# Attention phase: how fill products are paced, how much is kept for the next unit, and how VectorE's side list is ordered

## The chip, the cores and the metric

The kernel runs on one core of one Trainium2 chip. A core has TensorE (PE, matrix products; its weight loads are PEld), VectorE (DVE), ScalarE (ACT), GpSimd (POOL), SyncE (SP, which here issues DMAs), and DMA engines. The metric is device time in microseconds, the median of several runs. One further execution was profiled, and every duration below is from that one.

## The reference

Four sequences of 1024 tokens, 512 features, float32. Cut to what matters:

```python
x = x + xattn(layernorm(x), ctx, ctx)
x = x + ffn(layernorm(x))

# xattn: 16 heads of 32
q, k, v = heads(x @ Wq.T), heads(ctx @ Wk.T), heads(ctx @ Wv.T + bv)
scores = q @ k.T / sqrt(32)
mask = triu(ones, k=0); mask[0, 0] = False      # key s may be seen by queries t > s
probs = softmax(where(mask, -inf, scores))
out = (probs @ v) @ Wo.T + bo

# ffn: 128 experts each choose one token of every group of 32
logits = x @ controller + tie
perm = logits == max(logits over the 32 tokens)
out = combine(relu(dispatch(x, perm) @ f1 + bias) @ f2, perm)
```

The change lies in the first line, the attention. The expert part is left as it is.

## The kernel before

**Units.** `attention_phase` works in 16 units; a unit is one batch b and one group hc of four heads (u = 4 b + hc). The main loop (L581) runs u from -1 to 15. A round works on two units at once: it computes the scores of unit u+1, to find each query's maximum, and the softmax and output of unit u. A round has twelve steps k:

- `score_piece(u+1, k)` (L312; PE L325, masks L331): the scores of 128 queries against up to 512 keys, queries on the partitions, into two score buffers (tile sc); VectorE takes the negative maxima out of them (L337, tile nm). The pieces have 128, 256, 384, 512, 512, 128, 512, 256, 512, 384, 512, 512 columns.
- `key_block(u, k)` (L366; PE L381, L387): the same scores again, with keys on the partitions, into two score buffers (tile st), the maxima being subtracted by a product with a row of ones (L387, which reads mxT); ScalarE takes the exponential (L395, tile pr), GpSimd zeroes what is masked on the diagonal (L398). The blocks have 512, 384, 256, 128, then 512 four times, then 512, 384, 256, 128 queries. Here the first four belong to the first half of the queries, the other eight to the second.
- `weigh_values` (L422; PE L431, tile av), two steps behind: the probabilities times v.
- `add_sums` (L404): adds the probabilities up for the softmax's denominator, one half on GpSimd, the other on VectorE (L415, L418).
- At the end of a half of the queries `normalize` (L444): the denominator (pd, L449), its reciprocal on VectorE (L456), its spreading (pb, L460), and the multiplication into atT (L464).

There are three score buffers, so a score piece and a key block always wait for each other's readers. All other products share one PSUM buffer, ps_m.

**The maxima.** `split_maxima` (L341) writes the maxima as a sum of three bf16 numbers (five small VectorE operations, L348 to L353, and L345 first for the second half); PE then turns them (pmx, L358) and VectorE copies them to mxT (L361), which `key_block` reads. It is begun after piece 4 for the first half and after piece 11 for the second: VectorE's five operations are placed at once, and PE's turn becomes due 3.0 us later by the kernel's own reckoning.

**The fill.** Between score pieces and key blocks stand products for other units, each a generator that yields after every product of 0.86 us: q and k of unit u+2 (L207, L195), v of unit u+1 (L226), the rows of the output product of the batch before (L266, called o; VectorE adds the residual, L272), and in two of four rounds the turning of the next batch's normalized rows (L171, called x). They stand in one list, `fill`. `ensure` (L533) forces the list on until a named step is done, for example the q and k that the next piece reads. The planner keeps estimated clocks (`now`, `dve`, `act`, and `bank`, the time at which ps_m is free again). `slot` (L502) is called twice per step:

```python
owed[0] += credit                    # total of the round's fill / 24
while owed[0] > 0 or now[0] < until:
    if open_step[0] is None:
        if now[0] < bank[0]:
            return
        open_step[0] = choose(False)
```

So each round's fill is spread over its 24 slots, and nothing is meant to remain. The order that comes out is kept: the phase runs under a manual schedule for PE, VectorE, ScalarE and GpSimd. SP is not among them.

**The side list.** `aside` (L114) holds work for VectorE that is not urgent: the layer norm of the next batch (`measure`, L139 and L140, four times, an empty entry, then `center`, L150) and the moments of finished rows (`measure_row`, L254). Each step of a round takes one entry, whatever its length.

Of the kernel before, what the change touches and what calls it, by code (L numbers as in the profile page):

```python
# [14 lines left out]
ALU = mybir.AluOpType  # L15
# [22 lines left out]
def attention_phase(  # L38
# [74 lines left out]

    aside = deque()  # L114

    x_t = x.rearrange("b (h t p) d -> b h p t d", p=P, t=4)

    def ln_steps(b):
# [12 lines left out]
        def measure(half, i):  # L131
            if i == 0:
                stats[half] = (
                    spool.tile([P, 6], F32, tag="ln_stats", name=f"ln_stats_{b}_{half}"),
                    spool.tile([P, 4, 2], F32, tag="ln_mv", name=f"ln_mv_{b}_{half}"),
                    spool.tile([P, 4], F32, tag="ln_rstd", name=f"ln_rstd_{b}_{half}"),
                )
            st, mv, rstd = stats[half]
            nc.vector.bn_stats(st, held[half][:, i, :])  # L139
            nc.vector.bn_aggr(mv[:, i, :], st)  # L140
            given(dve, 1.0)
            if i == 3:
                nc.vector.tensor_scalar_add(rstd, mv[:, :, 1], EPS)
                nc.gpsimd.tensor_tensor(rstd, rstd, mhalf, ALU.pow)

        def center(t):
            half, i = divmod(t, 4)
            st, mv, rstd = stats[half]
            xn = qpool.tile([P, D], F32, tag="xn", name=f"xn_{b}_{t}")
            nc.vector.tensor_scalar(  # L150
                xn, held[half][:, i, :], mv[:, i, 0:1], rstd[:, i : i + 1],
                ALU.subtract, ALU.mult,
            )
            given(dve, 0.6)
            ready[t] = xn

        def prepare(half):
            for i in range(4):
                aside.append(lambda i=i: measure(half, i))
            aside.append(lambda: None)  # L160
            aside.append(lambda: center(4 * half))

        def step(t):
            while t not in ready:
                aside.popleft()()
            if t % 4 < 3:
                center(t + 1)
            xn = ready.pop(t)
            px = single([P, NC, P], f"px_{b}_{t}")
            for c in range(NC):  # L170
                nc.tensor.transpose(px[:, c, :], xn[:, ts(c, P)], ident)  # L171
            yield 4 * SMALL, act, 0.6
            nc.scalar.copy(xnTs[b][:, :, ts(t, P)], px)  # L173
# [68 lines left out]

    def load_residual(b, t):
        xt = opool.tile([P, D], F32, tag="xr", name=f"xr_{b}_{t}", bufs=3)
        nc.sync.dma_start(xt, x[b, ts(t, P), :])
# [6 lines left out]
    def measure_row(b, t, x2):  # L252
        st = opool.tile([P, 6], F32, tag="row_stats", name=f"row_stats_{b}_{t}", bufs=2)
        nc.vector.bn_stats(st, x2)  # L254
        nc.vector.bn_aggr(moments[:, b * NT + t, :], st)
        given(dve, 1.0)

    def o_step(b, t, ahead=None):
# [14 lines left out]
        nc.sync.dma_start(x2_dram[ds(b * S + t * P, P), :], xt)  # L273
        aside.append(lambda: measure_row(b, t, xt))

# [65 lines left out]
    def split_maxima(u, half):  # L341

        nm = nms.pop((u, half))
        if half == 1:
            nc.vector.tensor_tensor(nm[:, 0], nm[:, 0], nm[:, 1], ALU.min)  # L345
        mxs = mxs_tiles[half]
        n = nm[:, 0]
        nc.vector.tensor_copy(mxs[:, :, :, 0], n)  # L348
        rest = spool.tile([P, 4, R], F32, tag="rest", name=f"rest_{u}_{half}")
        nc.vector.tensor_tensor(rest, n, mxs[:, :, :, 0], ALU.subtract)  # L350
        nc.vector.tensor_copy(mxs[:, :, :, 1], rest)
        nc.vector.tensor_tensor(rest, rest, mxs[:, :, :, 1], ALU.subtract)
        nc.vector.tensor_copy(mxs[:, :, :, 2], rest)  # L353
        given(dve, 1.0)
        yield None
        pt = ps_m.tile([P, 4, P], BF16, tag="pm", name=f"pmx_{u}_{half}")
        for i in range(4):
            nc.tensor.transpose(pt[:, i, :], mxs[:, i].rearrange("p r m -> p (r m)"), ident16)  # L358
        yield 0.3, dve, 0.4
        mxT = spool.tile([P, HS], BF16, tag=f"mxT{half}", name=f"mxT_{u}_{half}", bufs=1 + half)  # L360
        nc.vector.tensor_copy(mxT, pt.rearrange("p i q -> p (i q)"))  # L361
        mxTs[u, half] = mxT

# [105 lines left out]


    fill, soon, done = deque(), deque(), set()
    open_step, owed = [None], [0.0]

# [5 lines left out]
    def advance(step):  # L479
# [4 lines left out]
        now[0] += part[0]  # L484
        owed[0] -= part[0]
        if len(part) == 1:
# [7 lines left out]
    def choose(force):  # L494
        for i in range(len(soon)):
            if soon[i][0] <= now[0] or (force and not fill):
                step = soon[i][1]
                del soon[i]
                return step
        return fill.popleft()[1] if fill else None  # L500

    def slot(credit, until=0.0):  # L502

        owed[0] += credit
        if owed[0] > 0 or now[0] < until:
            now[0] += TURN
        while owed[0] > 0 or now[0] < until:
            if open_step[0] is None:
# [13 lines left out]

    def named(steps, costs, *names):


        def noted(step, name):
            yield from step
            done.add(name)

        for step, cost, name in zip(steps, costs, names):  # L530
            fill.append((cost, noted(step, name)))

    def ensure(*names):  # L533
        while not done.issuperset(names):
            one_part()

    def begin(step, wait):

        next(step)
        soon.append((now[0] + wait, step))  # L540

# [11 lines left out]
    for half in range(2):  # L553
        ln_prepare(half)
        while aside:
            aside.popleft()()
        run(k_first[half])
# [14 lines left out]
    def add(kind, u, steps, cost=4 * LARGE, first=0):  # L572
        named(steps, [cost] * len(steps), *((kind, u, first + n) for n in range(len(steps))))

# [6 lines left out]
    for u in range(-1, NU):  # L581
# [6 lines left out]
        if b > 0:  # L588
            if hc == 0:
                load_residual(b - 1, 0)  # L590
            ends = (3, 6, 8, 8) if more else (2, 4, 8, 8)
            r0 = ends[hc - 1] if hc else 0
            rows = o_todo(b - 1, r0, ends[hc])
        if more and hc == 1:
            next_ln = ln_steps(b + 1)
            next_ln[0](0)
            aside.append(lambda: None)
            next_ln[1](0)
# [6 lines left out]
        elif more and hc == 2:  # L605
            ensure(("x", b + 1, 3))
            next_ln[0](1)
            aside.append(lambda: None)
            next_ln[1](1)
# [8 lines left out]
        else:  # L618
# [3 lines left out]
            add("o", b - 1, rows, first=r0)  # L622
        total = sum(cost for cost, _ in fill) + 4.0
        owed[0] = 0.0
        for k in range(STEPS):
            if u + 1 < NU:
# [3 lines left out]
                if k == 4:  # L630
                    begin(split_maxima(u + 1, 0), 3.0)
                if k == STEPS - 1:
                    begin(split_maxima(u + 1, 1), 3.0)
            weighed = False
            slot(total / (2 * STEPS), scores_free() if u >= 0 else 0.0)
            if u >= 0 and len(pending) == LAG and now[0] < scores_free():
                pending.popleft()()
                weighed = True
            if u >= 0:
                h, j = blocks[k]  # L640
                while (u, h) not in mxTs:
                    one_part()
                key_block(u, k)
            if sums:
                sums.popleft()()
            if aside:
                aside.popleft()()
            if len(pending) == LAG and not weighed:
                pending.popleft()()
            if u >= 0:  # L650
# [15 lines left out]
                pending.append(weigh)  # L666
            slot(total / (2 * STEPS), scores_free() if u + 1 < NU else 0.0)
    while sums:
# [3 lines left out]
    while soon or fill or open_step[0]:  # L672
        one_part()
    while aside:
        aside.popleft()()
    units.close()
# [387 lines left out]
```

## Time and profile before

| | us |
|---|---|
| three runs, median (lowest to highest) | 1543.44 (1539.7 to 1546.15) |
| the profiled execution, whole | 1544.16 |
| its span, first to last instruction | 1542.5 |
| mean granted TensorE clock | 0.961 |
| first score piece of the phase (L325) | 41.1 |
| last spreading of a denominator (L460) | 1204.1 |

From about 1206 us on the routing and the experts follow. Busy time by stage, from the windows view:

| stretch, us | PE busy | VectorE | ScalarE | GpSimd | PE clock |
|---|---|---|---|---|---|
| 200 to 400 | 190.11 | 117.65 | 63.29 | 69.36 | 0.97 |
| 400 to 600 | 195.56 | 119.13 | 60.36 | 75.79 | 0.97 |
| 600 to 800 | 197.15 | 117.14 | 58.84 | 73.90 | 0.99 |
| 800 to 1000 | 193.58 | 117.03 | 62.95 | 68.76 | 0.97 |
| 1140 to 1220 | 69.45 | 45.44 | 29.28 | 54.40 | 0.89 |

How to read the profile: busy time is the time in which an engine executes; matmuls are pipelined, so a busy PE is not PE at its peak. A row of the groups has line, engine, operation, tiles, count, then busy time and mean duration, then the idle time before and what ended it. The letter in front of an arrow is what was waited for.

### The profile page before, as it was taken

How to read it: one execution, taken by the hardware profiler on the slowest of the kernel's cores; microseconds unless marked ns; L12 is line 12 of the kernel's file. 1: busy time of each engine (PE TensorE's matmuls, PEld its weight loads, DVE VectorE, ACT ScalarE, POOL GpSimd, SP SyncE). 2: the span in 40 equal slices, each digit the busy share in tenths (PEclk: the TensorE clock that was granted, in tenths of full speed). 3: DMA queues.
4: the chain of work that ended last, by engine and by line, in shares of the span. 5: the costliest groups of instructions: out<-in, count | busy, mean ns of one | idle time of the engine just before them, and what ended most of it. 6: DMA issues, size and time to landing. Idle time of an engine off the chain costs nothing.

```text
span 1542.5 us, 32131 instructions
## 1 busy us (share of the span) xinstructions
PE 1449.4 (94%) x14048; PEld 780.1 (51%) x14048; DVE 897.8 (58%) x1353; ACT 516.7 (33%) x809; POOL 479.1 (31%) x557
## 2 busy tenths in 40 slices
PE   6999989999999999999999999999998898987996
PEld 4343444444353444453535443535443456877886
DVE  3655656655565655646665655565576454575664
ACT  1033333332322233232323332322235123644663
POOL 1033333432424232424242433342447410000222
PEclk9999989999999899999998999999999797898998
DMA  8000001000000210001011000000011669653664
GB/s 290 17 1 1 1 28 55 29 1 1 21 21 22 75 56 28 1 1 35 8 42 56 28 1 1 2 28 1 28 35 49 208 244 319 181 159 123 187 210 141
DMA packets 77868, 105.64 MB, mean 68 GB/s; under 512 B 4128, under 2 KB 41504, under 8 KB 77600
## 3 DMA queue, kind: packets, MB, share of 16 engines
q1 hardware_dynamic: 75168, 95.20, 19.2%
q0 software_dynamic: 2560, 8.39, 1.7%
q8 instruction: 110, 1.80, 0.5%
q14 instruction: 30, 0.25, 0.0%
HBM read 74.22 MB, written 29.36 MB: 67 GB/s over the span
## 4 chain that ended last, share of the span: by engine, by line
PE 80%; DVE 7%; issue 6%; POOL 3%; DMA 2%; ACT 1%; POOLq 0%; SPq 0%; ACTq 0%; DVEq 0%
PE sc L325 11%; PE st L381 10%; PE av L431 8%; PE pq L207 8%; PE pv L226 8%; PE pk L195 7%; PE po L266 6%; PE pd L862 3%; DVE nm L337 3%; PE sc L331 3%; PE pi L881 2%; PE st L387 2%; PE po L713 2%; PE pl L750 2%; PE pd L449 2%
## 5 line engine op out<-in xcount | busy, mean ns | idle before, releaser
L337 DVE TENSOR_REDUCE nm<-sc 128x2 f32<-128x1024 f32 (+3 forms) x384 | 349.5, 952 | 296.8 <-PE sc L331 210.3
L395 ACT ACTIVATE pr<-st 128x1024 f32<-128x1024 f32 (+3 forms) x384 | 290.4, 808 | 587.4 <-PE st L387 577.0
L398 POOL TENSOR_SCALAR_AFFINE_SELECT pr<-pr 128x256 f32<-128x256 f32 x256 | 113.6, 452 | 469.3 <-ACT pr L395 467.7
L418 POOL TENSOR_TENSOR acc<-acc,pr 128x1024 f32<-128x1024 f32 (+3 forms) x128 | 209.2, 1634 | 115.0 <-ACT pr L395 106.9
L325 PE MATMUL sc<-kT,qT 32*128 32x512 f32 (+3 forms) x1536 | 202.0, 537 | 7.4 <-ACT pr L395 5.4
L381 PE MATMUL st<-qT,kT 32*128 32x512 f32 (+3 forms) x1536 | 196.8, 551 | 0.0
L431 PE MATMUL av<-pr,v 128*32 128x512 f32 (+3 forms) x1536 | 168.7, 508 | 6.4 <-POOL pr L398 6.0
L195 PE MATMUL pk<-ct,w_k 128*128 128x512 f32 x256 | 125.6, 620 | 9.2 <-DMA w_k<-in_wkT_dram 9.2
L226 PEld LDWEIGHTS pv<-w_v,ct 128*128 128x128 f32 x1024 | 118.7, 192 | 26.4 <-issue 13.3
L207 PE MATMUL pq<-xnT,w_q 128*128 128x512 f32 x256 | 128.3, 627 | 1.4 <-ACT xnT L173 1.4
L226 PE MATMUL pv<-w_v,ct 128*128 128x128 f32 x1024 | 128.3, 280 | 0.0
L381 PEld LDWEIGHTS st<-qT,kT 32*128 32x128 f32 x1536 | 67.5, 188 | 116.2 <-issue 89.5
L418 DVE TENSOR_TENSOR acc<-acc,pr 128x1024 f32<-128x1024 f32 (+3 forms) x128 | 119.6, 935 | 10.3 <-POOL pr L398 9.1
L325 PEld LDWEIGHTS sc<-kT,qT 32*128 32x128 f32 x1536 | 73.9, 186 | 101.0 <-issue 58.3
L415 POOL TENSOR_TENSOR acc<-pr,pr 128x768 f32<-128x768 f32 (+1 forms) x32 | 67.6, 2111 | 117.7 <-ACT pr L395 117.7
L979 POOL DMA_DIRECT2D out_dram<-xr x32 | 24.3, 758 | 253.4 <-DVE xr L978 253.1
L266 PE MATMUL po<-w_o,atT 128*128 128x512 f32 x192 | 94.9, 615 | 0.0
L195 PEld LDWEIGHTS pk<-ct,w_k 128*128 128x128 f32 x256 | 45.0, 192 | 71.1 <-issue 65.7
L431 PEld LDWEIGHTS av<-pr,v 128*32 128x32 f32 x1536 | 32.0, 109 | 88.7 <-issue 64.4
L207 PEld LDWEIGHTS pq<-xnT,w_q 128*128 128x128 f32 x256 | 45.5, 197 | 56.5 <-issue 51.8
L387 PE MATMUL st<-mxT,ones 32*128 32x512 bf16 (+3 forms) x768 | 72.9, 328 | 0.0
L456 DVE RECIPROCAL rd<-pd 128x128 f32<-128x128 f32 x32 | 30.5, 954 | 52.8 <-PE pd L449 52.8
(94 smaller groups left out, 1601.9 us busy)
## 6 DMA issues: line engine op xcount, KB each, us to landing
ct<-in_ctxT_dram SPq DMA_DIRECT2D x8, 1024.0 KB, 5.2
xt<-in_x_dram SPq DMA_DIRECT2D x8, 1024.0 KB, 5.3
xr<-in_x_dram SPq DMA_DIRECT2D x32, 256.0 KB, 2.6
xn_dram<-x SPq DMA_DIRECT2D x8, 1024.0 KB, 5.3
xn<-xn_dram SPq DMA_DIRECT2D x8, 1024.0 KB, 6.2
f<-in_f_dram SPq DMA_DIRECT2D x16, 512.0 KB, 4.3
xr<-x_dram SPq DMA_DIRECT2D x32, 256.0 KB, 4.4
f<-in_f_dram SPq DMA_DIRECT2D x32, 256.0 KB, 4.9
```

The source lines that it names most:

```text
L195: nc.tensor.matmul(pk, lhsT=weights["k"][:, c, ts(hc, P)], rhs=cts[b, half][:, c, :], start=(c == 0), stop=(c == NC - 1),)
L207: nc.tensor.matmul(pq, lhsT=weights["q"][:, c, ts(hc, P)], rhs=xnTs[b][:, c, ts(half, HS)], start=(c == 0), stop=(c == NC - 1),)
L226: nc.tensor.matmul(pv[:, t, :], lhsT=cts[b, half][:, c, ts(t, P)], rhs=weights["v"][:, c, ts(hc, P)], start=(c == 0), stop=(c == NC - 1),)
L266: nc.tensor.matmul(po, lhsT=atTs[b * NC + c][:, ts(t, P)], rhs=weights["o"][:, c, :], start=(c == 0), stop=(c == NC - 1),)
L325: nc.tensor.matmul(scs[r // 2][:, r % 2, :n], lhsT=qT[rr, ts(i, P)], rhs=kT[rr, ds(c0, n)], start=True, stop=not diag,)
L337: nc.vector.tensor_reduce(nm[:, c0 // HS, i % 4, ts(g, 2)], scs[g][:, :, :n], AX.X, ALU.max, negate=True)
L381: nc.tensor.matmul(scs[r // 2][:, r % 2, :n], lhsT=kT[rr, ts(j, P)], rhs=qT[rr, ds(h * HS + q0, n)], start=True, stop=False,)
L387: nc.tensor.matmul(scs[r // 2][:, r % 2, :n], lhsT=ones16[rr, :], rhs=mxT[rr, ds(q0, n)], start=False, stop=True,)
L395: nc.scalar.activation(pr[:, :, :n], scs[g][:, :, :n], AF.Exp)
L398: nc.gpsimd.affine_select(out=d, in_=d, compare_op=ALU.is_ge, fill=0.0, base=0 if j == 0 else -1, pattern=[[0, 2], [P + 1, P]], channel_mu ...
L418: engine.tensor_tensor(acc, acc, pr[:, :, :n], ALU.add)
L431: nc.tensor.matmul(avs[u, h][rr, q0:], lhsT=vs[u][:, j, rr], rhs=pr[r // 2][:, r % 2, : HS - q0], start=(j == 0), stop=(j == last),)
```

## The change

It touches the planner and the places in which VectorE's small work stands.

- `slot` gets the number of slots left in the round. It works on until the backlog of fill has shrunk by its share of what lies above a reserve of 5.0 us. The reserve stays in the list for the next round. The backlog is counted down product by product.
- Entries of the side list carry a name and a cost. `beside(0.9)` takes entries until their cost is 0.9 us or more, `finish` does named ones at once. The empty entries between the x load and its first measure are gone.
- The split of the maxima becomes two entries of the side list (0.9 and 0.7), put at its front. The second makes PE's turn due, 1.5 us later. Before a key block both are finished.
- A row's moments go to the front of the list; they are finished before the residual load that reuses their buffer.
- In the last batch's rounds the rows of the output product are spread as (2, 4, 7, 8) instead of (2, 4, 8, 8): one row moves to the last round.

```diff
-    aside = deque()
+    aside, pieces_left = deque(), {}
+
+    def later(name, cost, work, front=False):
+        pieces_left[name] = (cost, work)
+        if front:
+            aside.appendleft(name)
+        else:
+            aside.append(name)
+
+    def finish(*names):
+        for name in names:
+            if name in pieces_left:
+                cost, work = pieces_left.pop(name)
+                work()
+                given(dve, cost)
+
+    def beside(budget):
+        while aside and budget > 0:
+            name = aside.popleft()
+            if name in pieces_left:
+                budget -= pieces_left[name][0]
+                finish(name)
...
         def prepare(half):
             for i in range(4):
-                aside.append(lambda i=i: measure(half, i))
-            aside.append(lambda: None)
-            aside.append(lambda: center(4 * half))
+                later(("m", b, half, i), 1.0, lambda i=i: measure(half, i))
+            later(("pow", b, half), 1.0, lambda: None)
+            later(("c", b, half), 0.6, lambda: center(4 * half))
...
         def step(t):
-            while t not in ready:
-                aside.popleft()()
+            half = t // 4
+            finish(*(("m", b, half, i) for i in range(4)), ("c", b, half))
...
     def load_residual(b, t):
+        finish(("row", b, t - 3), ("row", b - 1, t + 5))
...
-        aside.append(lambda: measure_row(b, t, xt))
+        later(("row", b, t), 0.9, lambda: measure_row(b, t, xt), front=True)
...
     def split_maxima(u, half):
...
+        def first_two():
+            if half == 1:
+                nc.vector.tensor_tensor(n, n, nm[:, 1], ALU.min)
+            nc.vector.tensor_copy(mxs[:, :, :, 0], n)
+            nc.vector.tensor_tensor(rest, n, mxs[:, :, :, 0], ALU.subtract)
+            nc.vector.tensor_copy(mxs[:, :, :, 1], rest)
+
+        def third():
+            nc.vector.tensor_tensor(rest, rest, mxs[:, :, :, 1], ALU.subtract)
+            nc.vector.tensor_copy(mxs[:, :, :, 2], rest)
+            soon.append((now[0] + 1.5, turn()))
...
+        later(("split", u, half, 1), 0.7, third, front=True)
+        later(("split", u, half, 0), 0.9, first_two, front=True)
...
-    def slot(credit, until=0.0):
-
-        owed[0] += credit
-        if owed[0] > 0 or now[0] < until:
+    def slot(slots_left, until=0.0):
+
+        goal = backlog[0] - max(0.0, backlog[0] - RESERVE) / slots_left
+        if backlog[0] > goal or now[0] < until:
             now[0] += TURN
-        while owed[0] > 0 or now[0] < until:
+        while backlog[0] > goal or now[0] < until:
...
-            ends = (3, 6, 8, 8) if more else (2, 4, 8, 8)
+            ends = (3, 6, 8, 8) if more else (2, 4, 7, 8)
...
                 if k == 4:
-                    begin(split_maxima(u + 1, 0), 3.0)
+                    split_maxima(u + 1, 0)
                 if k == STEPS - 1:
-                    begin(split_maxima(u + 1, 1), 3.0)
+                    split_maxima(u + 1, 1)
...
-            slot(total / (2 * STEPS), scores_free() if u >= 0 else 0.0)
+            slot(2 * (STEPS - k), scores_free() if u >= 0 else 0.0)
...
                 h, j = blocks[k]
+                finish(("split", u, h, 0), ("split", u, h, 1))
                 while (u, h) not in mxTs:
                     one_part()
                 key_block(u, k)
             if sums:
                 sums.popleft()()
-            if aside:
-                aside.popleft()()
+            beside(0.9)
...
-            slot(total / (2 * STEPS), scores_free() if u + 1 < NU else 0.0)
+            slot(2 * (STEPS - k) - 1, scores_free() if u + 1 < NU else 0.0)
```

`turn`, not shown, is the former second half of `split_maxima`, unchanged: the four transposes and the copy to mxT.

## The prediction

> **What bounds the kernel now.** I read the page first. Its first section has TensorE (PE) busy for 94% of the span; the chain of waits gives PE 80%. PE is the bound of the attention phase (0 to about 1206 us), which is all that the change touches, so only time in which PE does nothing useful can be won or lost.
>
> ```profile
> PE 1449.4 (94%) x14048; PEld 780.1 (51%) x14048; DVE 897.8 (58%) x1353; ACT 516.7 (33%) x809; POOL 479.1 (31%) x557
> PEclk9999989999999899999998999999999797898998
> ```
>
> The digits of PEclk below 9 are the first hint: in places the granted clock drops. Next I asked for PE's waits between 41 and 1206 us ("us in total, times, longest").
>
> ```profile
> PE pmx L358 <- DVE mxs L353: 10.2, 7, 2.6
> PE av L431 <- POOL pr L398: 6.0, 5, 1.8
> PE sc L325 <- ACT pr L395: 5.4, 9, 0.7
> PE px L171 <- ACT xnT L173: 4.7, 7, 0.7
> PE px L171 <- DVE xn L150: 3.3, 1, 3.3
> PE px L171 <- DVE mxT L361: 2.3, 3, 0.9
> ```
>
> The costliest is the turn of the split maxima (pmx) waiting for VectorE's split (mxs). Those waits bring another loss, seen in the windows view (busy time by engine, then the clock):
>
> ```profile
> 651.26:654.67 3.41, 1.56 (x28) 0.92 (x24) 3.31 (x6) 0.09 (x1) 2.60 (x4) 1.00 0.01 2
> 654.67:658.09 3.42, 3.42 (x21) 1.17 (x14) 1.22 (x4) 0.39 (x1) 0.00 (x0) 0.50 0.02 5
> ```
>
> After a stretch in which PE was busy for 1.56 of 3.41 us, the next 3.41 us run at half clock. Last, the timeline shows losses that no wait line carries. Here a key block (st) is followed at once by a score piece (sc):
>
> ```profile
> 316.12 1.14 PE L381 MATMUL st<-qT,kT 32*128 32x512 f32 x8
> 317.30 0.60 PE L325 MATMUL sc<-kT,qT 32*128 32x256 f32 x4
> 318.58 0.30 PEld L325 LDWEIGHTS sc<-kT,qT 32*128 32x128 f32 x4 [1.08 <-ACT pr L395]
> 318.58 0.70 PE L325 MATMUL sc<-kT,qT 32*128 32x256 f32 x4 [0.68 <-ACT pr L395]
> ```
>
> Only half of the piece's matmuls start; the others wait until the exponential has emptied a score buffer. I measured every such group from its start to the start of the next one, less what its columns take undisturbed (0.43 us for 512 fp32 columns, from L195) and less 0.21 that each group loses even with full cover. By that, units 0 to 13 lose 82 us: pmx waits and the half clock behind them 23.0, runs of turned x rows 16.0, the half clock behind those 5.5, behind the start 1.5, and the rest, 36, in thin gaps: a score piece and a key block with under 0.8 us of other PE work between them.
>
> **What the change does to the order.** I compared the two kernels' instruction orders. PE has the same work and practically as many breaks between kinds (919 stretches against 917), so cutting fill work into single products costs nothing by itself. The removed and added host code has no instruction. POOL (525) and SP (208) keep their counts. What moves is where fill stands, and where VectorE does its side work.
>
> **1. The split maxima.** Direct waits, start to start, are 1.59, 0.97, 2.80, 0.97, 2.02, 0.97 and 2.02: 11.3 us. In the six half-clock stretches behind them (from 139, 354, 539, 655, 839 and 955 us) the groups take 11.7 us more than at full clock. In the new order each pmx stands a block or more behind its split, with 2 to 4 us of PE work between, against 0.43 of VectorE for the second part (L352, L353 at their shortest, 0.19 and 0.20, with the gaps). So -23.0.
> Here a rule is weighed. The Trainium skill, "TensorE: Matmul & The Clock Gate", section "HAM oscillation", asks for no PE-idle gaps over about 3.4 us. By it none of these seven waits would cost clock, the removal would be worth 11.3, and the sum below would be about 9 us worse (half-clock terms -11.7 and +3.0 fall away). The rows above show half clock behind a 2.02 us wait, so I take the rows.
> What is late next: in units 5, 6, 9, 10 and 13 the pmx of the second half now stands right before the key block that needs it, as score piece 4, pmx, weighing, key block 4. On VectorE its copy (mxT, L361, 0.42) stands behind both reductions of piece 4 (L337 with 1024 elements, 1.22 each). Units 6 and 10: when piece 4 ends, VectorE is 1.0 behind (reductions of piece 3 2.44, L464 0.68, add 0.63, measure 0.94, against 3.8 of PE), so the copy is done after 1.0+2.45+0.42+0.1=3.95, and the block's products with the maxima end at 4.2; with cover they would end at 0.31+0.57+1.29=2.17. That is 2.0 each. Units 5 and 9, where the split and a measure pile up, 2.5; unit 13, with no measure, 1.1. Together 10.1. Between 0 (VectorE ahead) and 16 (another 1 us behind). Such a wait and the next thin gap share a 3.4 us stretch, so I put half clock behind about two of the five, at 1.4 each as after the old waits: 3.0. Net of part 1: -9.9.
>
> **2. Forced runs.** Keeping 5 us for the next unit meets `ensure`, which demands some of it at once. At the end of units 5 and 9 the order is now twelve o products (three rows) and four x turns in a row, through one ps_m buffer. An x turn waits 0.84 for its copy (506.02, 507.35, 508.68 in the timeline: 1.33 apart, 0.43 of work); a row of o waits about 0.95, the same with an addition of 0.69 in place of a copy of 0.59. 3x0.95+3x0.84=5.4 against 4.6 now. Unit 1: four k products and four x turns, 3.4 against 6.8 now. Units 7 and 11 get x, k, q, score piece in one run: 3x0.84=2.5 each, new; unit 3 0.85, new. Total 20.1 against 16.0: +4.1, and +1.0 of half clock.
>
> **3. Thin gaps.** Priced from the trace by kind, times the counts in both orders (units 0 to 13): key block to piece of 256 with nothing between, 1.28: 5 to 7; with pmx alone between, 0.67: 3 to 7. To a piece of 128, nothing between, 1.20: 1 to 5. From a block of 256 to a piece of 512, 0.86: 2 to 6. From one of 128, 0.38: 6 to 8. Score piece to key block with only a weighing between, 0.1 to 0.9: 19 to 13. With the other small kinds 33.2 to 43.4: +10.2. Blocks with nothing between rise from 15 to 26, since fill is held back while ps_m is taken by pmx, pd or pb. Three blocks without fill now follow each other in units 1, 2, 5 and 9; following VectorE's durations there it falls 1 to 1.5 behind and the next key block loses more than its price: up to 6.8 in all, nothing if the old prices hold; I take 4.0. Part 3: +14.2.
>
> **4. The side list and the queues.** VectorE's measures come one block earlier (the empty entries are gone). The first of unit 2 stands about 2.2 us into the unit; its x half lands 5.3 us after its issue (211.9 to 217.25 in the DMA issues), some 2.7 into the unit. Up to 0.5 of VectorE, beside PE's work: 0. If uncovered, one thin gap more, 0.8. The residual load now comes behind `finish` of the row that frees its buffer, which only fixes VectorE's order: 0. On SP the x load of the second half stands behind three stores and loads in units 5 and 9, and its first measure comes only in block 2: 0.
>
> **5. The end.** Row 7 of batch 2 goes to the last unit and the kept products follow: 12 o products instead of 2 stand behind the last score piece. 10x0.86=8.6 leave the units before. Behind it, the way to key block 5, which starts POOL's chain of additions (3.2 us each at 1180 to 1201 us, PE waiting for L398), grows from 17.0 to about 21.4; four of the products, forced right after pb, then hold back block 6, so POOL idles some 2.2. -8.6+6.6=-2.0. All hidden it would be -8, none hidden 0.
>
> **Sum:** -9.9+4.1+1.0+14.2-2.0=+7.4. Against the profiled execution's own 1544.16 us (span 1542.5) that gives 1551.5, rounded to **1552 us**; that execution lies 0.7 above the median of 1543.44, well within the three runs.
>
> **Rivals.**
> A, faster: the waits for the maxima go with their half clock and nothing of like size comes, because VectorE runs ahead of PE. For it: VectorE is busy only 58%, and one pmx copy takes 0.42. Against it: VectorE's order is fixed, and the copy does stand behind two reductions. Then part 1 is -23.0+4, and parts 2, 3 and 5 give +5, +8 and -3: -9, **1535**.
> B, a wash: the reserve is spent in forced runs, and what pmx gains the gaps give back; with a third of part 3 gone, +2.7: **1547**.
> C, clearly slower: the place is VectorE in the blocks without fill. Once it is over 1 us behind, key blocks and pieces wait on each other; all of part 3's 6.8, part 1's 16 with half clock behind all five (7), and nothing hidden at the end: +7.4+2.8+6+4+2, **1566**. It decides if the excess behind piece 4 is over 3 us.
>
> **Chances.** Forecast 0.45 (its own range 1548 to 1558), A 0.15, B 0.22, C 0.18. A measurement of this kernel can tell about 0.5%, 7.7 us, from no change. Faster by more: A alone, 0.13. Within: B, a third of the forecast and a trace of A, 0.39. Slower: the rest, 0.48. The range from 1535 to 1565 leaves the far ends of A and C out.
>
> **What will show it.** Part 1: no L358 <- L353 among PE's waits, and the half-clock stretches at unit starts gone except behind x turns; in units 5, 6, 9, 10, 13 a key block 4 over 2 us from start to next start. Part 2: 0.8 to 1 us between the o rows before the x turns at the ends of units 5 and 9, and in units 7 and 11 before k, q and score piece 4. Part 3: L325 <- L395 well above 5.4 us. Part 5: o products between the key blocks of unit 15, a later start of POOL's chain, and a shorter stretch from the first score piece of the last round to the end of the phase. The forecast is wrong if key block 4 starts its products with the maxima at once, or if the 26 bare gaps cost well under their 0.4 to 1.3 us each.

## The result and the profile after

The changed kernel takes 1566.3 us (median of 4 runs, 1563.1 to 1570.2) against 1541.6 for the kernel before in the same comparison: a ratio of 1.0163, 95% interval 1.0138 to 1.0188. It is slower, as forecast, but by about 25 us where 8 were forecast. The profiled execution took 1570.2 us (span 1568.5).

The page of the changed kernel, PE's row and the granted clock in 40 slices:

```profile
PE 1463.1 (93%) x14048; PEld 786.1 (50%) x14048; DVE 896.8 (57%) x1353; ACT 516.6 (33%) x809; POOL 478.9 (31%) x557
PEclk9999999999999899999998999999999797898999
```

Same instructions, same engines; PE is only "busier" because records last longer. The digits of PEclk have changed little either, so the page alone does not tell where 25 us went. The attention phase does: counted to the start of its last single product that spreads a denominator (pb), it ends at 1229.9 us in place of 1205.8, 24.1 later. What follows it has the same code and took 338.6 us against 336.7. So nearly all of the loss is where the change is.

PE's waits in that phase (us in total, times, longest):

```profile
PE sc L346 <- ACT pr L426: 10.4, 14, 1.0
PE px L192 <- ACT xnT L194: 6.1, 9, 0.7
...
PE px L192 <- DVE xn L171: 3.9, 3, 1.3
PE po L287 <- DVE xr L293: 3.2, 4, 0.8
...
PE st L418 <- DVE mxT L389: 1.7, 5, 0.3
```

The leading wait of before (pmx on mxs, 10.2) is gone from the head of the list; 0.9 is left of it. What has grown is the score piece waiting for an exponential (L325 before, L346 now): 5.4 became 10.4. New are o products waiting for their row's addition. The last line is key block 4 waiting for the copy of the maxima, and it looks harmless: 0.3 at a time. The block as a whole is not, as the timeline of unit 6 shows (start, duration, engine, line, tiles, count, then the idle time before and what ended it):

```profile
532.57 1.48 PE L346 MATMUL sc<-kT,qT 32*128 32x512 f32 x8
533.98 0.40 PE L384 MATMUL pmx<-ident,mxs 128*128 128x128 bf16 x4
534.31 0.64 PE L462 MATMUL av<-pr,v 128*32 128x256 f32 x8
534.88 2.12 PE L412 MATMUL st<-qT,kT 32*128 32x512 f32 x8
537.33 0.40 PE L418 MATMUL st<-mxT,ones 32*128 32x512 bf16 x4 [0.33 <-DVE mxT L389]
537.54 0.40 PE L346 MATMUL sc<-kT,qT 32*128 32x128 f32 x4
538.89 0.80 PE L346 MATMUL sc<-kT,qT 32*128 32x128 f32 x4 [0.95 <-ACT pr L426]
```

This is the row that the forecast named: score piece 4, pmx, weighing, key block 4. The eight fp32 products show 2.12 us; undisturbed they show 1.14. So this row of the timeline, which merges the eight, is about 1 us too long without showing a wait, and 0.33 stand in the wait behind it. From start to next start, the block takes 2.66 where its columns and a normal switch take 1.29: 1.4 lost. Then comes a bare step, that is, a key block followed at once by a score piece with no fill between; it waits 0.95 more. What the hidden 1 us waits for stands in the row of PE's weight loads (PEld) for the second half of the block, and VectorE's rows give the times:

```profile
535.87 0.19 PEld L412 LDWEIGHTS st<-qT,kT 32*128 32x128 f32 x2 [0.70 <-DVE nm L358]
533.81 0.68 DVE L161 BATCH_NORM_STATS2 ln_stats<-xt 128x6 f32<-128x512 f32 x1
534.53 0.18 DVE L162 BATCH_NORM_AGGREGATE ln_mv<-ln_stats 128x2 f32<-128x6 f32 x1
534.62 2.32 DVE L358 TENSOR_REDUCE nm<-sc 128x2 f32<-128x1024 f32 x2
536.86 0.41 DVE L389 COPY mxT<-pmx 128x512 bf16<-128x512 bf16 x1
```

The copy stands behind piece 4's two reductions, as forecast. But it accounts for the smaller part. The block's first two heads start at once, in the one free score buffer; the other two need a buffer that piece 4 holds, and start at 535.87, when the first of the two reductions has ended. So the heads run two and two in place of all four together, which is the hidden 1 us. The copy, done at 537.27, adds some 0.4. Only a weighing stands between piece 4 and the block; in e1 below, with k products there, both waits are gone. What was not forecast at its size comes next, in the windows view (length, then busy time of PE, PEld, DVE, ACT and POOL, and the granted clock):

```profile
535.29:538.70 3.41, 2.32 (x16) 0.70 (x12) 2.82 (x7) 0.88 (x1) 0.00 (x0) 1.00 0.00 0
538.70:542.12 3.42, 3.23 (x18) 3.00 (x19) 1.80 (x6) 1.06 (x2) 0.00 (x0) 0.50 0.02 5
542.12:545.53 3.41, 3.41 (x16) 2.02 (x19) 0.00 (x0) 0.00 (x0) 0.00 (x0) 0.50 0.00 0
```

The waits and the bare step fall into one stretch, and two stretches at half clock follow. Five units have this row (5, 6, 9, 10 and 13), and in the first four the same happens: half clock from 446.5, 538.7, 760.6 and 856.1 us, 20.4 us of it. The phase as a whole is not longer at half clock than before: up to the last 30 us, the stretches add up to 44.3 us in place of 51.2. The six behind the old waits for the split are gone, and these have come in their place.

### The profile page after: what moved, and what is told of

The parts are those of the page before. It is cut to its first block, busy times and chain, and to the rows that moved or that the text cites. A ratio compares the mean times of both kernels' runs of the same rounds, so it can differ in the third digit from the quotient of the medians.

```text
span 1568.5 us, 32127 instructions
## 1 busy us (share of the span) xinstructions
PE 1463.1 (93%) x14048; PEld 786.1 (50%) x14048; DVE 896.8 (57%) x1353; ACT 516.6 (33%) x809; POOL 478.9 (31%) x557
## 4 chain that ended last, share of the span: by engine, by line
PE 80%; DVE 7%; issue 7%; POOL 2%; ACT 2%; DMA 1%; POOLq 0%; SPq 0%; DVEq 0%; ACTq 0%
PE sc L346 11%; PE st L412 10%; PE pv L247 8%; PE av L462 8%; PE pq L228 8%; PE pk L216 8%; PE po L287 6%; DVE nm L358 4%; PE pd L887 3%; PE sc L352 3%; PE st L418 2%; PE pi L906 2%; PE po L738 2%; PE pl L775 2%; PE pd L480 2%
## 5 line engine op out<-in xcount | busy, mean ns | idle before, releaser
L346 PE MATMUL sc<-kT,qT 32*128 32x512 f32 (+3 forms) x1536 | 207.6, 534 | 17.3 <-ACT pr L426 10.4
L247 PEld LDWEIGHTS pv<-w_v,ct 128*128 128x128 f32 x1024 | 122.3, 196 | 33.4 <-issue 23.1
L247 PE MATMUL pv<-w_v,ct 128*128 128x128 f32 x1024 | 133.6, 285 | 0.0
L449 DVE TENSOR_TENSOR acc<-acc,pr 128x1024 f32<-128x1024 f32 (+3 forms) x128 | 126.3, 987 | 9.3 <-POOL pr L429 9.2
L346 PEld LDWEIGHTS sc<-kT,qT 32*128 32x128 f32 x1536 | 76.2, 185 | 109.8 <-issue 50.3
L253 DVE TENSOR_TENSOR v<-pv,bv_sb 128x512 f32<-128x512 f32 x32 | 22.1, 690 | 83.5 <-PE pv L247 83.5
```

Source lines behind the costliest of these rows:

```text
L247: nc.tensor.matmul(pv[:, t, :], lhsT=cts[b, half][:, c, ts(t, P)], rhs=weights["v"][:, c, ts(hc, P)], start=(c == 0), stop=(c == NC - 1),)
L346: nc.tensor.matmul(scs[r // 2][:, r % 2, :n], lhsT=qT[rr, ts(i, P)], rhs=kT[rr, ds(c0, n)], start=True, stop=not diag,)
L449: engine.tensor_tensor(acc, acc, pr[:, :, :n], ALU.add)
```

## The experiments

All figures are medians; the ratio is to the kernel before on the same chip in the same comparison. "Attention" is the end of that phase in the profiled execution, which leaves out what follows with the same code in every kernel. It is a single execution each: the changed kernel, profiled twice (e9), differs by 5.7 us there.

| kernel | time us | ratio (95% interval) | attention us | behind it us |
|---|---|---|---|---|
| before | 1541.6 | 1 | 1205.8 | 336.7 |
| changed | 1566.3 | 1.0163 (1.0138 to 1.0188) | 1229.9 | 338.6 |
| e1 maxima ahead | 1558.2 | 1.0079 (1.0048 to 1.0109) | 1215.8 | 338.7 |
| e2 no reserve | 1561.4 | 1.0111 (1.0054 to 1.0168) | 1225.9 | 339.6 |
| e3 old split | 1551.9 | 1.0050 (1.0035 to 1.0066) | 1207.7 | 339.4 |
| e4 old pacing | 1533.6 | 0.9926 (0.9901 to 0.9952) | 1186.5 | 341.1 |
| e5 clock kept, twice | 1566.8 | 1.0148 (1.0123 to 1.0172) | 1219.7 | 348.3 |
| e6 side list alone | 1544.5 | 1.0005 (0.9989 to 1.0020) | 1203.6 | 338.8 |
| e7 maxima ahead, no reserve | 1545.1 | 1.0005 (0.9992 to 1.0019) | 1207.0 | 341.6 |
| e8 clock kept, once | 1559.6 | 1.0091 (1.0072 to 1.0110) | 1216.4 | 341.0 |
| e9 changed, again | 1574.5 | 1.0182 (1.0158 to 1.0205) | 1235.6 | 338.5 |
| e10 e4, o rows last | 1519.5 | 0.9822 (0.9803 to 0.9841) | 1176.8 | 338.0 |
| e11 e7, o rows last | 1538.8 | 0.9948 (0.9927 to 0.9968) | 1201.1 | 341.8 |

**e1: the turn of the maxima demanded ahead of score piece 4**

```diff
                     ensure(("q", u + 1, k // 4), ("k", u + 1, k // 4))
+                if k == 4 and u >= 0:
+                    finish(("split", u, 1, 0), ("split", u, 1, 1))
+                    while (u, 1) not in mxTs:
+                        one_part()
                 score_piece(u + 1, k)
```

> The changed kernel, but at the start of each round's score piece 4 the turn of the second half's maxima and its copy (mxT) are demanded first, so that the copy stands on VectorE ahead of piece 4's two reductions. The reserve, the pacing and the side list stay. Bare steps from a key block to a score piece fall from 26 to 14. Theory 1 (the largest loss is key block 4 waiting for the copy queued behind piece 4's reductions, with the half clock behind it and the bare gap that follows): some 24 us go, 1540 to 1547, and the half-clock stretches of units 5, 6, 9 and 10 go with it. Theory 2 (the reserve and the runs it forces at a round's end are the loss): these stay, so at most 5 us go, 1561 to 1567. Theory 3 (single products and their pacing lose all over, in thin gaps): 1555 to 1563.

14.1 us of the attention phase went, not 24. The place of the loss was right, for the half-clock stretches behind key block 4 went with the move (what is left, from 506.3, 574.5 and 813.5 us, stands at the ends of units 5, 6 and 9, behind x turns). But the demand brings a run of its own. PE in unit 6 of this kernel:

```profile
528.89 3.84 PE L247 MATMUL pv<-w_v,ct 128*128 128x128 f32 x32 [0.71 <-DVE atT L495]
533.51 0.38 PE L384 MATMUL pmx<-ident,mxs 128*128 128x128 bf16 x4 [0.78 <-DVE v L253]
533.82 1.14 PE L346 MATMUL sc<-kT,qT 32*128 32x512 f32 x8
534.89 1.98 PE L216 MATMUL pk<-ct,w_k 128*128 128x512 f32 x4
536.81 1.14 PE L412 MATMUL st<-qT,kT 32*128 32x512 f32 x8
```

The v step that was open in the one ps_m buffer had to be finished first: 0.71 and 0.78 of new waits. (The st row is 1.14 here; that is the undisturbed value used above.) The half clock went as theory 1 said, but the whole time, 1558.2, lies in the range of theory 3. And with the turn out of the way, k products now stand between score piece 4 and key block 4. They cover the wait for the score buffer too, so e1 does not tell that wait from the one for the copy; e7 does.

**e2: no reserve** (`RESERVE = 0.0`)

> The changed kernel with a reserve of 0 in place of 5 us: each round spreads all its fill over its own slots and leaves nothing for the next. Five units still have score piece 4, turn, weighing and key block 4 in a row. Theory 1 (the copy of the maxima behind piece 4): no gain, 1562 to 1572. Theory 2 (reserve and forced runs): the forced o rows, x turns, and x-k-q runs go, 12 to 18 us, 1548 to 1554. Theory 3 (pacing of single products): within 5 us of 1566, as the pacing rule stays.

4.0 us of the attention phase, no more than one kernel's executions differ, and a ratio whose interval overlaps that of the changed kernel. Theory 2, by which the reserve and its forced runs are the loss, falls as the main cause: without a reserve units 5 and 9 still end with twelve o products and four x turns, and units 7 and 11 still force an x turn, k and q.

**e3: the split of the maxima as before, all else as changed** (`begin(split_maxima(...), 3.0)` with the seven operations in one piece)

> The changed kernel with the split of the maxima as before: all of it at once after the last piece of a half, and its turn due a fixed 3.0 us later by the planner's clock. Pacing, reserve and side list stay as changed. Theory 1 (the copy of the maxima behind piece 4): the wait of key block 4 in units 5, 6, 9 and 10 goes (24), and the turns' waits for the split come back with half clock behind them (12 to 20): 1554 to 1563. Theory 2 (reserve and forced runs): nothing of the loss goes and the old waits of 23 come on top: 1580 to 1590. Theory 3 (pacing all over): the same as theory 2, some 1578 to 1588.

Better than any theory gave it: 1207.7, only 1.9 behind the kernel before. So under the changed pacing the changed split costs 22 us.

**e4: the pacing as before, split and side list as changed**

```diff
-        goal = backlog[0] - max(0.0, backlog[0] - RESERVE) / slots_left
+        owed[0] += credit
...
-            slot(2 * (STEPS - k), scores_free() if u >= 0 else 0.0)
+            slot(total / (2 * STEPS), scores_free() if u >= 0 else 0.0)
```

> The kernel before's pacing (each slot gets the same credit, no reserve, the rows of o shared out as before) with the changed split of the maxima and the changed side list. The turn of the second half's maxima stands ahead of score piece 4 everywhere. Theory 1 (the copy of the maxima behind piece 4, brought by the pacing): 23 us of old waits go, a few come in thin gaps: 1525 to 1540, faster than before. Theory 2 (reserve and forced runs): the same, since there is no reserve. Theory 3' (the side list's new order on VectorE is the loss): 1558 to 1568.

Faster than the kernel before, and inside the range of theories 1 and 2. The waits of pmx for mxs are gone, and no half clock is left between 212 and 1177 us. Theory 3' falls.

**e6: the changed side list alone, with PE's order as before**

> The kernel before with the changed side list alone: pacing and the split of the maxima are as before, and PE's order is that of the kernel before, instruction by instruction. Only VectorE's side work moves (measures without the empty entries, split by duration). As predicted in part 4 (worth nothing): 1540 to 1547. If the side list is what makes the version with the old pacing fast: 1530 to 1537, and the changed split is then worth nothing. If the side list loses: 1549 or more.

No difference: the list is worth nothing by itself, and so the split is worth 1203.6 - 1186.5 = 17 us under the old pacing. The four corners of attention's end, in us, all with the changed side list (the pacing here includes how the rows of o are shared out in the last batch):

| | old split | changed split |
|---|---|---|
| old pacing | 1203.6 | 1186.5 |
| changed pacing | 1207.7 | 1229.9 |

The split gains 17 or costs 22; the pacing costs 4, which is within the spread, or 43. The ratios of the whole times say the same: 1.0005 and 0.9926 in the first row, 1.0050 and 1.0163 in the second. Neither part loses the time by itself: they meet. The orders show where. In units 5, 6, 9 and 10 the turn of the second half stands no later than behind score piece 0 with the old split under either pacing, behind piece 2 with the changed split and the old pacing, and behind piece 4 with both changes. Why so late is read from the planner and not tested by itself: slots that always place a little keep ps_m taken, and the turn is due later.

**e5 and e8: PE kept at work during key block 4's wait.** The fp32 products of key block 4 in units 5, 6, 9 and 10 are repeated (the repeats overwrite the same values, so only time changes), twice in e5 and once in e8:

```diff
-        for r in range(R):
+        again = 1 if k == 4 and u in (5, 6, 9, 10) else 0
+        for n_th, r in enumerate([*range(R)] * (1 + again)):
...
-                rhs=qT[rr, ds(h * HS + q0, n)], start=True, stop=False,
+                rhs=qT[rr, ds(h * HS + q0, n)], start=True, stop=n_th < R * again,
```

> The changed kernel, but key block 4 of units 5, 6, 9 and 10 computes its kT-qT products three times over (the second and third overwrite the same values), so that PE works through the wait for the copy of the maxima: 2 x 4 matmuls, 1.7 us of PE work per block, 6.9 us of useless work in all. The place of the copy stays. Theory 1 (the wait of 1.4 to 2.2 us puts these units into half clock): the work fits into the wait (some 0.6 to 1.5 us of it may not), and the half-clock stretches from 446.5, 538.7, 760.6 and 856.1 us go or shrink: 6 to 9 us less than the changed kernel, 1557 to 1561. Rival (the half clock comes from the x turns and o runs in these units, not from this wait): 0 to 4 us more, 1566 to 1570.

> As the run that kept the clock, but key block 4 of units 5, 6, 9 and 10 repeats its kT-qT products once in place of twice: 0.86 us of useless work per block, 3.4 in all. The last run ended the attention phase 10.2 us earlier than the changed kernel (1219.7 against 1229.9), but the phase behind it, whose code is the same, took 348.3 us against 338.6, so that the time hardly moved. Theory 1 (this wait puts the units into half clock): the attention phase ends again before 1225. If the longer second phase was no effect of the kept clock: it takes 336 to 342 again as in all other runs, and the time is 1557 to 1562. If a clock that is kept early is paid back by the phase behind it: 345 or more again, and 1565 to 1568.

With useless work added the attention phase is 10.2 us (e5) and 13.5 us (e8) shorter. In the four units themselves it is 6.7 and 11.4; most of the rest lies in units 2 and 3, whose order is unchanged. First the changed kernel around key block 4 of unit 5, then e8 around the same block:

```profile
443.13:446.54 3.41, 2.12 (x21) 0.98 (x16) 1.93 (x6) 1.77 (x2) 0.00 (x0) 1.00 0.00 0
446.54:449.95 3.41, 3.41 (x7) 1.37 (x5) 1.80 (x6) 0.16 (x1) 0.00 (x0) 0.50 0.03 5
440.48:443.90 3.42, 2.44 (x24) 1.29 (x24) 2.29 (x6) 1.26 (x2) 0.00 (x0) 1.00 0.00 0
443.90:447.31 3.41, 3.41 (x18) 1.57 (x20) 1.80 (x6) 0.67 (x1) 0.00 (x0) 1.00 0.02 5
```

The repeat covers 0.86 of the 1.4 us, the block ends no earlier, the bare step behind it is still there, and the clock stays full. Units 5, 6, 9 and 10 together last 320.8 us in place of 332.2, although each does 0.86 us more work. So what is won is clock, not waiting.

A rival has to be weighed for part of this. The clock changes only at the borders of a fixed grid of stretches of 3.41 us, and in another run a block lies elsewhere on it. In units 6 and 10 of e8 the block and the bare step fall into two stretches (unit 6: 529.23 to 532.64, and on to 536.06). By the count of product work in the last section each has enough without the repeat. There the place alone would have kept the clock. In units 5 and 9 the stretch holds the repeat, and without it would have had about as little work as the stretches that lost the clock.

e8's whole time follows the attention phase (1.0091 against 1.0163, and 1.0182 for the changed kernel beside it) and lies in the range of theory 1. e5's does not: the phase behind took 348.3 us, and the whole time, 1566.8, lies in the rival's range. By the rule written ahead of e8, a kept clock that is paid back later would have shown 345 or more again; it showed 341.0. So the longer second phase belongs to e5 alone, and why all five of its executions took that long (1565.4 to 1570.0) stays open.

**e7: e1 and e2 together**

> The changed kernel with the turn of the maxima demanded ahead of score piece 4 and, beside that, no reserve. What it leaves of the changed pacing is the rule itself: single products, shared out by what is left. Theory 2' (with the maxima out of the way, the reserve is the rest of the loss): the forced runs go, and it comes within 5 us of the version with the old pacing, 1533 to 1540. Theory 3 (the rule itself loses: more breaks between kinds and more thin gaps): it stays near the version with the maxima ahead, 1550 to 1560.

It lies between: 22.9 us of attention's 24.1 are back (14.1 and 4.0 alone), but the old pacing with the same split is still 20.5 faster. Half of that, 9.8, is in units 7 and 11, which still begin their second half with a forced run.

e7 also settles what key block 4 waits for. In unit 6 the copy is made ahead of piece 4's reductions (525.68 to 526.07) and only a weighing stands between piece 4 and the block:

```profile
524.53 1.14 PE L346 MATMUL sc<-kT,qT 32*128 32x512 f32 x8
525.60 0.64 PE L462 MATMUL av<-pr,v 128*32 128x256 f32 x8
526.17 1.78 PE L412 MATMUL st<-qT,kT 32*128 32x512 f32 x6
528.53 1.72 PE L247 MATMUL pv<-w_v,ct 128*128 128x128 f32 x13
527.25 0.19 PEld L412 LDWEIGHTS st<-qT,kT 32*128 32x128 f32 x2 [0.78 <-DVE nm L358]
```

The block takes 2.36 from start to next start, so 1.1 of the 1.4 is still lost, to the score buffer (0.9 in unit 5). What no longer follows is a bare step: fill stands behind the block, and there is no half clock.

**e9: the changed kernel once more**

> The changed kernel itself, beside the others on one chip, for a second look at what does not change: attention phase to 1229 to 1231 us, the phase behind it 336 to 342 us, time 1563 to 1569.

1235.6, 5.7 later than the first time, and the time is 1574.5: both outside what was expected; the phase behind, 338.5, is inside. All of the 5.7 arises ahead of unit 5 (which starts at 425.4 in place of 418.0, and itself gives 1.7 back), with half clock from 63.2 and 76.8 us, which the first profile does not have. From unit 6 on the two agree unit by unit. This is what the spread of the runs looks like from within.

Unit 5 is the telling one. Key block 4 and the bare step behind it lose the same there as in the first profile (2.67 from start to next start, and the same wait of 0.95), but they lie across a border of the grid:

```profile
448.87:452.28 3.41, 3.08 (x24) 1.00 (x16) 3.37 (x7) 0.11 (x1) 0.00 (x0) 1.00 0.01 2
452.28:455.69 3.41, 2.46 (x14) 1.37 (x14) 1.84 (x8) 1.83 (x2) 0.00 (x0) 1.00 0.02 5
```

No half clock follows: the same order with the same waits costs clock in one execution and none in the other.

**e10 and e11: x turns ahead of the o rows.** In the second and third unit of a batch the fill list gets what the next round demands first (the x turns, and in the third unit the second halves of k and q), and the rows of o, which nothing demands soon, last:

```diff
-            add("o", b - 1, rows, first=r0)
             add("x", b + 1, [next_ln[2](t) for t in range(4)], 4 * SMALL)
+            add("o", b - 1, rows, first=r0)
...
-            add("o", b - 1, rows, first=r0)
             add("x", b + 1, [next_ln[2](t) for t in range(4, NT)], 4 * SMALL, first=4)
             add("k", u + 2, k_todo[1:], first=1)
             add("q", u + 2, q_todo[1:], first=1)
+            add("o", b - 1, rows, first=r0)
```

> The version with the old pacing and the changed split and side list (1533.6 us), with another order of fill in the second and third unit of a batch: the x turns, which the next round demands, come ahead of the rows of o, which nothing demands soon. Four x turns in a row at the end of units 5 and 9 are spread over four gaps, and bare steps from a key block to a score piece fall from 21 to 19. If what is demanded soonest must come first: 6 to 12 us less, 1522 to 1528. If the x turns lose as much where they are spread (a gap filled by a turn of 0.43 us is thin too): 1532 to 1536.

> The same order of fill in the version with the changed pacing, the maxima ahead and no reserve (1545 us). The forced run of an x turn, four k and four q products ahead of score piece 4 in units 7 and 11 becomes one of four q products, but bare steps rise from 23 to 27. If the forced runs are what parts this version from the old pacing (10 of its 20 us): 1533 to 1540. If it is the thin gaps that the rule leaves all over: 1543 to 1550.

e10, on top of e4, is the best version: 0.9822 of the kernel before, 1519.5 us (below the range given), and 9.7 us of attention better than e4. For what changed, first the end of unit 5 in the changed kernel:

```profile
500.53 3.70 PE L287 MATMUL po<-w_o,atT 128*128 128x512 f32 x8 [0.84 <-DVE xr L293]
505.07 0.66 PE L192 MATMUL px<-ident,xn 128*128 128x128 f32 x4 [0.84 <-DVE xr L293]
506.40 0.66 PE L192 MATMUL px<-ident,xn 128*128 128x128 f32 x4 [0.68 <-ACT xnT L194]
507.74 0.93 PE L192 MATMUL px<-ident,xn 128*128 128x128 f32 x4 [0.68 <-ACT xnT L194]
```

Then the same x turns in e10:

```profile
476.88 1.14 PE L346 MATMUL sc<-kT,qT 32*128 32x512 f32 x8
477.95 0.66 PE L192 MATMUL px<-ident,xn 128*128 128x128 f32 x4
478.54 1.06 PE L462 MATMUL av<-pr,v 128*32 128x512 f32 x8
479.53 0.71 PE L412 MATMUL st<-qT,kT 32*128 32x256 f32 x8
480.07 0.29 PE L418 MATMUL st<-mxT,ones 32*128 32x256 bf16 x4
481.01 0.63 PE L192 MATMUL px<-ident,xn 128*128 128x128 f32 x4 [0.66 <-ACT pr L426]
```

In a row, each turn waits 0.68 for the last one's copy out of the same buffer. Spread, the copies have score pieces and blocks to hide behind. Not every wait goes: the turn at 486.09 us still waits 1.30 for its centred row. In the four units 5, 6, 9 and 10 the time beyond work and normal switches falls from 31 (e4) to 22 us. e11 gains 5.9 by the same edit, in the range that stands for the forced runs being the difference; units 7 and 11 lose 4.4 each in place of 7.6.

## Why the prediction was off

The direction was right, and the places of the loss were mostly the ones named; the sum was too small. In attention +24.1 was measured and +7.4 forecast (which assumed the rest unchanged; it took 1.9 more). The steps that failed are terms of the sum: the half clock behind key block 4 was put at 3.0 us and took 8.0; x turns in neighbouring slots were put at 1.3 and took 7.4; the end was put at -2.0 and came to +0.2; and two small kinds of gap were put at nothing and took 4.6. By the forecast's parts, with losses measured group by group as there:

**Part 1, the old waits: right.** -23.0 was forecast for the seven waits and their half clock. The wait row fell from 10.2 to 0.9, and under the old pacing the split alone brings 17. The rule weighed there, from the Trainium skill, "TensorE: Matmul & The Clock Gate", section "HAM oscillation", asks for no PE-idle gaps over about 3.4 us, and by it none of these waits would have cost clock. The rows contradict it: in the stretch from 535.29 us no idle time of PE is over 0.95 us, and half clock follows. The rows were the right choice.

**Part 1, key block 4: right in place, too large in size, and right in only a part of its cause.** Forecast 2.5 in units 5 and 9, 2.0 in 6 and 10, 1.1 in 13, together 10.1. Measured: 1.4 in each of the first four and 0.6 in 13; in units 5 and 9 another 0.8 ahead of it, where pmx waits 0.43 for the split; together 7.8. The forecast charged it all to the copy behind the two reductions. The copy does end last, but the score buffer that piece 4 holds takes 1.0 of the 1.4, and e7 loses about that with the copy out of the way.

**Part 1, the half clock behind it: the first term that failed.** "I put half clock behind about two of the five, at 1.4 each ... 3.0." It came in four of five, and in two of these for two stretches: 8.0 us. e8 confirms the order of size by taking the cause away (11.4 us in the four units, of which about 2.7 lie in stretches behind x turns that got shorter too, and in units 6 and 10 the place on the grid helped). The prediction had itself noted that such a wait and the next thin gap share a stretch; having seen it, it should have counted every place where both stand together. Even so the count would have been a chance and not a certainty: the same place in unit 5 cost no clock in e9.

**Part 2, forced runs: right.** The o rows show 0.84 where 0.95 was said, and the x turns cost what they did before. In units 7 and 11 the run of x, k and q loses 0.78, 0.74 and 0.76 behind its three kinds, 2.3 against 2.5; its start in unit 7:

```profile
601.15 0.66 PE L192 MATMUL px<-ident,xn 128*128 128x128 f32 x4 [0.71 <-DVE atT L495]
602.48 1.98 PE L216 MATMUL pk<-ct,w_k 128*128 128x512 f32 x4 [0.67 <-ACT xnT L194]
```

**Part 3, thin gaps: the second term that failed, and the largest miss.** The counts held (26 bare steps), and the units with only such gaps (4, 8, 12, 13) came out within 1 us. But x turns in neighbouring slots were priced with the small kinds, some 1.3 us in all, as if one turn could fill a gap. A second turn in the next slot waits for the first one's copy, for its own centred row, or for both:

```profile
582.06 0.27 PE L418 MATMUL st<-mxT,ones 32*128 32x128 bf16 x4
583.63 0.63 PE L192 MATMUL px<-ident,xn 128*128 128x128 f32 x4 [1.29 <-DVE xn L171]
```

This one, in unit 6, loses 1.4, and six such places (units 2, 6, 7, 10 and 11) lose 7.4 us. Nor were two smaller kinds counted: at the ends of units 3, 7 and 11 the last k products stand right ahead of the score piece that needs them (0.74 each), and q or x behind a block of 128 columns loses 0.79, three times.

**Part 4, the side list: right.** Nothing (e6).

**Part 5, the end: the third term that failed.** -8.6 leave the work ahead of the last score piece, as said. The stretch behind it grew by 8.8 (45.7 to 54.5), not 6.6: key block 5 starts at 21.7 as forecast (21.4), but the four forced products hold the next block back by 4.0 (7.2 us in place of 3.2 between them), where 2.2 was said. Net 0.2, not -2.0.

Together: 5.0 for the half clock, 6.1 for the x turns, 2.2 for the end, 4.6 for these two smaller kinds, 0.8 for half clock elsewhere, less 2.3 for key block 4: 16.4 of the 16.7 that were missing.

Rival C had the time, 1566, but by luck, for its condition did not hold: it was to decide if the excess behind piece 4 passed 3 us, and that was 1.4 to 2.2. What it had right was half clock behind nearly every such wait and no gain at the end.

One thing the sum could not show: it added parts 1 to 3 as if they were independent. By the four corners the split is good or bad according to the pacing beside it.

## What to carry to other kernels

A wait that is short by itself must be priced together with the next gap: if both fall into one stretch of about 3.4 us, the half clock behind them can cost as much as the waits (8.0 us against 7.8 here). Ask how much product work such a stretch has left, not how long its longest gap is. A wait that one row names may hide behind another: see what each half of a group waits for. In a filler order, put first what is demanded soonest and leave for last what nothing waits for; and where one buffer serves all fill, spread the small pieces, for two in neighbouring slots wait for each other. When two parts of a change decide one order together, test the four corners before giving either a price.

## What the runs showed of the hardware

Half-clock stretches begin and end on a grid in every trace: those of the changed kernel from 446.54 and 538.70 us lie 92.16 apart, 27 times 3.413. So an idle time of the same length can cost clock or not, by where it falls, as unit 5 shows in the changed kernel's two executions.

A busy PE is not a measure of this: 2.32 of 3.41 us busy was followed by half clock and 2.44 in e8 was not, and the former contains most of the row in which the heads run two and two (2.12 in place of 1.14). The work of the products is a measure. Count 0.43 us for 512 fp32 columns, half of that for bf16, and a quarter where four heads share the array (a covered key block of 512 queries is then 0.86 + 0.22, and with the switch of 0.21 the measured 1.29). By this estimate the stretches of key block 4 that lost the clock hold 0.90, 0.97, 1.19 and 0.86 us of work; that of unit 5 in e9, which kept it, 1.40; those of units 5 and 9 in e8 1.67. Over the attention phases of all thirteen traces, from 72 us on: of 63 stretches at full clock with under 1.2 us of work, 61 were followed by half clock; of 46 with 1.2 to 1.4, 16; of 4083 with 1.4 or more, none.

Work that is thrown away can pay: 3.4 us of repeated products made the changed kernel about 0.9% faster, beside itself on one chip (1.0091 against 1.0182).

The time behind the attention phase, with the same code, was 336.7 to 341.8 us in twelve profiled executions and 348.3 in one. That spread, with the half clock at the start in e9, is as large as the effects looked for, so the attention phase was compared by itself.
